# Two graph-attention layers on one core: the planner's durations taken from the profile, layer 0's mask turned over by four transfers instead of one, the last attention but one kept for the end

## The chip, the core and the metric

The kernel runs on one core of a Trainium2 chip. The core has five engines with queues of their own: TensorE (PE, matrix products; its weight loads are shown apart as PEld), VectorE (DVE), ScalarE (ACT), GpSimd (POOL) and SyncE (SP, which here only issues transfers). They meet through semaphores. The metric is the time of one execution on the device, in microseconds (us), of this one core; lower is better.

## What is computed

32 graphs, each with 512 nodes and 512 features per node, and an adjacency matrix of 512 x 512 integers, drawn sparse. Everything is float32. Two layers, each with a layernorm and a relu ahead and a residual after:

```python
h = relu(layernorm(x))                        # layer 0
s = leaky_relu(h @ w_src[:, None] + (h @ w_dst)[None, :] + attn_b, 0.2)
attn = softmax(where(adj + eye == 0, -inf, s), axis=-1)
x = x + attn @ h

h = relu(layernorm(x))                        # layer 1
mask = (adj > 0) | eye
h = elu(gat(h, mask, W1, a_src1, a_dst1, b1, heads=4))   # 512 -> 4 x 256
x = x + gat(h, mask, W2, a_src2, a_dst2, b2, heads=1)    # 1024 -> 512
```

A `gat` projects (`xl = x @ W`), forms `leaky_relu(xl.a_src + xl.a_dst)` for each pair of nodes and each head, sets pairs outside the mask aside, takes the softmax over the sources and multiplies with `xl`.

## The kernel before

**Tiles.** 512 nodes are four tiles of 128 rows. A graph has one layer-0 attention, a projection with W1, four heads' attentions, an elu, a projection with W2 and a last attention. Each projection is made of seven products of half-size blocks instead of eight (`products`, L848 to L915): sums of blocks are formed ahead on DVE or POOL (`combine`, L881/L882), each product is 128 x 257 or 258 in a bank of PSUM (`acc`), and is copied out by ACT or DVE (`evict`, L539/L541 on ACT, L545/L547 on DVE: the writes to `pair` and `xl`) or added to what is there by DVE (L913). The weights carry two more columns with the sums W.a, made at the start (L384 the dot products on DVE, L488 sums on POOL), so that a projection also yields the scores.

**An attention.** Its weights are made in `edge_weights` (L634 to L676). For every tile of 128 rows: the largest neighbour's score of each row (L643, on DVE, 128 x 512, with a mask), then the bound of the row's exponent, `z` (L649) and `m` (L651), both 128 x 4. PE turns that `m` over to lie along a row and spreads it (`spread`, L506, `acc<-ident,col`), ACT forms the leaky relu (L665), DVE subtracts `m` (L668), POOL adds the mask (L671), ACT takes the exponential (L674), PE aggregates (L684). For this each mask is needed twice, with sources in rows and with sources in columns: `m0` and `m0T`, `m1` and `m1T`. Scores of 4, 8 or 16 rows go through PE (L605), are copied to a row, stored in DRAM (`lines`, L611) and read back spread to all partitions (`row_of`, L621; L631 puts a row into a bank).

**Masks.** `masks0` (L751) loads the adjacency by POOL's queue (L725), adds the unit matrix (L758), makes it 0 or a large negative (L761), and turns it over by `transposed_mask` (L729, issue at L735 on SP's queue). `transposed_mask(m, mT, whole)` does it by one transfer when `whole`, else by four, one per tile of rows. The one transfer leaves the result in the order tile, block, column, and `mask_row` (L745) therefore reads it with a stride; four transfers put blocks `mT[:, :, t]` in place, and rows are read without. `masks1` is the like for layer 1.

**The order of work.** Nothing is ordered by hand. The functions record operations in a `Plan`: engine or engines to choose from, a cost (occupied, there) in ns for each, and what is read and written. `Plan.run` (L90) makes list schedules (`draft`), in which each engine takes the operation of the best rank that is due; buffers of limited number (`slots`, L325 on) and a lock between DVE and POOL hold operations back. It tries several weights of looking ahead, derives ranks from the latest times of a schedule, makes the next, and keeps the schedule that ends first by its own costs. All engines then issue in that order. So a cost that is changed can change the whole order and the engine an operation runs on, while the operations stay the same. The costs are in `on_pe` to `by_turning` (L235 to L268) and beside single operations.

**The main program** (L1074 to L1111) records graph 0's and 1's layer 0 first with the constants, then for each graph the masks, the projection, the last attention of the graph before, the heads, the next graph's layer 0 and the second projection. `EARLY` says how many of the four tiles of the last attention but one are recorded ahead of the last projection.

Of the kernel before, what the change touches and what calls it, by code (L numbers as in the profile page):

```python
# [245 lines left out]

def on_act(n, per_partition=0):

    one = n / 1.2 + (95.0, 140.0, 280.0)[per_partition]
    return one, one + 60.0  # L250


def on_pool(n, narrow=False):
# [15 lines left out]
def kernel(  # L269
# [24 lines left out]
    nc = tc.nc  # L294
    B, N, D = x.shape
    H, F = att_src1.shape
# [6 lines left out]
    W2 = (2 + D) // 2  # L303
# [136 lines left out]
    def scores_1(att):  # L440
        for k in range(KD):
            for h in range(H):
                q, kk = QUARTER[k // (KD // 2)][h % 2], k % (KD // 2)
                for i in range(2):
                    op(
                        "DVE", on_dve(F),
                        lambda w=w1_s[q][:, kk, h // 2, :], i=i, h=h: dot(
                            w[:, 2:], flat(att[0])[:, i * HF + h * F : i * HF + (h + 1) * F], w[:, i : i + 1]
                        ),
                        W["w1"]((q, kk)) + att[0](i), W["w1"]((q, kk, h // 2, i)), -LATER, lock=True,  # L450
                    )

    def scores_2(att):
        part = const.tile([P, KH, 2], F32, name="part")
        for k in range(KH):
            (q, r), kk = QUARTER[k // (KH // 2)], k % (KH // 2)
            lo, hi = w2_s[q][:, kk, :], w2_s[r][:, kk, :]
            for i in range(2):
                op(
                    "DVE", on_dve(W2),  # L460
                    lambda lo=lo, i=i, k=k: dot(lo[:, 2:], flat(att[1])[:, i * D : i * D + W2 - 2], part[:, k, i : i + 1]),
                    W["w2"]((q, kk)) + att[1](i), W["w2"](("part", k)), -LATER, lock=True,
                )
                op(
                    "DVE", on_dve(W2),
                    lambda lo=lo, hi=hi, i=i: dot(hi, flat(att[1])[:, i * D + W2 - 2 : (i + 1) * D], lo[:, i : i + 1]),
                    W["w2"]((r, kk)) + att[1](i), W["w2"]((q, kk, i)), -LATER, lock=True,
                )
            op(
                "DVE", on_dve(2), lambda lo=lo, k=k: nc.vector.tensor_add(lo[:, :2], lo[:, :2], part[:, k, :]),  # L470
                W["w2"]((q, kk, 0), (q, kk, 1), ("part", k)), W["w2"]((q, kk, "a")), -LATER,
            )
# [62 lines left out]
    def evict(src, dst, src_of, dst_of, n, bias=None, psum_half=False):  # L535

        def by_act():
            if bias is None:
                nc.scalar.copy(dst_of(), src_of())  # L539
            else:  # L540
                nc.scalar.activation(dst_of(), src_of(), AF.Identity, bias=bias)  # L541

        def by_dve():
            if bias is None:
                nc.vector.tensor_copy(dst_of(), src_of())  # L545
            else:
                nc.vector.tensor_scalar(dst_of(), src_of(), -1.0, None, op0=ALU.add)  # L547

        op(("ACT", "DVE"), (on_act(n, bias is not None), on_dve(n)), (by_act, by_dve), src, dst)

    def turned(values_of, src, place, results_of, dst):

        e = Buffer("row")
        op(
            "ACT", (1040.0, 1100.0),
            lambda: nc.scalar.copy(
                e.at.bitcast(U16).rearrange("p (b f) -> p b f", b=2), values_of().bitcast(U16).rearrange("p (f b) -> p b f", b=2)
            ),  # L560
            src + place, e(0),
        )
        op(
            "SP", by_turning(4 * P * N),
            lambda: nc.sync.dma_start(
                values_of().bitcast(U16).rearrange("p (c n) -> p c n", n=P), e.at.bitcast(U16), transpose=True
            ),
            e(0), src,
        )

        def pair():
            out = results_of()
            k, t = out.shape[1], out.shape[2]
            nc.scalar.copy(
                out.bitcast(U16).rearrange("p k t (n b) -> p k t n b", b=2),
                values_of().bitcast(U16).rearrange("p (b t k n) -> p k t n b", b=2, k=k, t=t),
            )

        op("ACT", (1160.0, 1220.0), pair, src, dst)

    def spread(part, col_of, ahead):

# [51 lines left out]
    def edge_weights(kind, scores, ac, lines, k, mask_max, mask, near):  # L634


        a_of = lambda t: ac.at[:, k, t : t + 1]
        a_row = spread(scores, a_of, AHEAD) if lines is None else in_bank(row_of(lines, k))
        amax, z, m = Buffer("col"), Buffer("col"), Buffer("col")
        for t in range(T):  # L640
            op(
                "DVE", on_dve(N + 60),
                lambda t=t: nc.vector.tensor_tensor_reduce(  # L643
                    by_blocks(junk), mask_row(mask_max, t), by_blocks(a_row.at), 1.0, LOWEST, ALU.add, ALU.max,
                    accum_out=amax.at[:, t : t + 1],
                ),
                a_row(*ROW) + mask_max(*ROW), amax(t),
            )
        op("DVE", on_dve(T), lambda: nc.vector.tensor_add(z.at, ac.at[:, k + 1, :], amax.at), scores + amax(*ROW), z(0))  # L649
        op(  # L650
            "DVE", on_dve(T), lambda: nc.vector.scalar_tensor_tensor(m.at, z.at, SLOPE, z.at, op0=ALU.mult, op1=ALU.max),  # L651
            z(0), m(0),
        )

        E = Buffer(kind)
        m_row = (
            spread(m(0) + E("place"), lambda t: m.at[:, t : t + 1], AHEAD) if near
            else in_bank(row_of(in_lines(lambda: m.at, m(0), 1), 0))
        )
        c_of = lambda t: ac.at[:, k + 1, t : t + 1]  # L660
        c_row = spread(scores + E("place"), c_of, AHEAD) if lines is None else row_of(lines, k + 1)
        for t in range(T):
            op(
                "ACT", on_act(N, 1),
                lambda t=t: nc.scalar.activation(E.at[:, t, :], c_row.at, AF.Prelu, bias=a_of(t), scale=1.0, alpha=SLOPE),  # L665
                c_row(*ROW) + scores, E(t),
            )
            op("DVE", on_dve(N), lambda t=t: nc.vector.tensor_sub(E.at[:, t, :], E.at[:, t, :], m_row.at), m_row(*ROW) + E(t), E(t))  # L668
            op(
                "POOL", on_pool(N, True),  # L670
                lambda t=t: nc.gpsimd.tensor_add(by_blocks(E.at[:, t, :]), by_blocks(E.at[:, t, :]), mask_row(mask, t)),  # L671
                E(t) + mask(*ROW), E(t), lock=True,
            )
            op("ACT", on_act(N), lambda t=t: nc.scalar.activation(E.at[:, t, :], E.at[:, t, :], AF.Exp), E(t), E(t))  # L674
        return E
# [42 lines left out]
    def load_adj(b, m):  # L718

        first, early = not START.wrote, len(adj_loads) < 3
        adj_loads.append(b)
        op(
            "POOL", (1100.0, 5500.0) if first else (2200.0, 16000.0 if early else 8000.0), lambda: nc.gpsimd.dma_start(m.at, node_tiles(adj, b)),  # L725
            () if first else START(0), m(*ROW) + (START(0) if first else []),
        )

# [15 lines left out]

    def mask_row(mask, t):  # L745

        if mask.kind in ("m0T", "m1T"):
            return mask.at.rearrange("p a (b n) -> p a b n", n=P)[:, :, t, :]
        return by_blocks(mask.at[:, t, :])

    def masks0(b):  # L751


        m0, m0T = Buffer("m0"), Buffer("m0T")
        load_adj(b, m0)
        for t in range(T):
            own = lambda t=t: m0.at[:, t, node_block(t)]
            op("DVE", on_dve(P), lambda own=own: nc.vector.tensor_add(own(), own(), ident), m0(t), m0(t), lock=True)  # L758
        op(
            "DVE", on_dve(T * N, 4.0),  # L760
            lambda: nc.vector.tensor_scalar(m0.at, m0.at, 0.0, NO_EDGE, op0=ALU.is_equal, op1=ALU.mult),  # L761
            m0(*ROW), m0(*ROW), lock=True,
        )
        transposed_mask(m0, m0T, True)
        return m0, m0T

    def masks1(b):
# [18 lines left out]
    def layer0_scores(b):  # L786
        rstd, nmr = layernorm(X[b])
        h0, ac = Buffer("h"), Buffer("ac")
        for t in range(T):
            relu_normed(h0, X[b], t, rstd, nmr)  # L790
            for i, w in ((1, ws_r), (0, wd_r)):
                op(
                    "DVE", on_dve(D), lambda t=t, w=w, i=i: dot(h0.at[:, t, :D], w, ac.at[:, i, t : t + 1]),
                    h0(t) + W["w0"](0, 1), ac((i, t)), lock=True,
                )
        c = ac(*((1, t) for t in ROW))
# [274 lines left out]

    EARLY = 1  # L1074
    load_x(0)
    att = load_constants()
    layer0_scores(0)
# [61 lines left out]
```

## Time and profile before

| | us |
|---|---|
| median of three runs | 3646.97 (3645.85 to 3647.93) |
| profiled execution, its own time | 3648.51 |
| its span in the profile | 3646.7 |
| PE busy (matmul instructions 16852) | 3542.6, 97% |
| PE weight loads | 3036.1, 83% |
| DVE busy | 2851.2, 78% |
| ACT busy | 2264.6, 62% |
| POOL busy | 1424.6, 39% |
| matmuls of the attentions, L684 | 920.4 + 491.2 + 447.9 in their three largest groups |

The mean clock that PE was granted is 0.994 of full. An engine's line in the profile says when its instructions ran, and a wait names the instruction of another engine (or the transfer) that released it. A busy share is a mean over the whole run. The run has a start of some 150 us, in which constants are loaded and the first graph has no other to work beside, then graphs of about 110.8 us each that look alike, and an end of some 100 us without further graphs.

### The profile page before, as it was taken

The numbers are of one execution on the slowest core, as the hardware profiler recorded it, in microseconds if no ns is written. First come the engines' busy times: TensorE is split into PE (matmuls) and PEld (weight loads), VectorE is DVE, ScalarE is ACT, GpSimd is POOL, SyncE is SP. The second block draws the span as 40 slices with busy tenths as digits, with TensorE's granted clock in tenths as the row PEclk, the third lists the DMA queues.
The fourth block names the chain that finished last, engine by engine and source line by source line (L and its number), as shares of the span: only waits on it lengthen the run. The fifth ranks groups of instructions, "written<-read, shape, count | busy, mean of one in ns | idle before, by whom it ended". The sixth has DMA issues, their size and how long they took to land.

```text
span 3646.7 us, 50543 instructions
## 1 busy us (share of the span) xinstructions
PE 3542.6 (97%) x16852; PEld 3036.1 (83%) x16852; DVE 2851.2 (78%) x7367; ACT 2264.6 (62%) x3929; POOL 1424.6 (39%) x1279
## 2 busy tenths in 40 slices
PE   4899999999999999999999999999999999999998
PEld 3788888888888888888888888888888888888887
DVE  7978778877778877778787788877787877887755
ACT  2666566665666665666666667655666656666554
POOL 4534334434334343334343344343343433343422
PEclk9999999999999999999999999999999999999999
DMA  6244433444433444334443334443334443344321
GB/s 172 77 105 119 104 92 104 100 121 113 96 96 103 104 121 112 90 96 105 115 116 98 95 103 99 125 116 86 97 110 105 119 108 89 103 103 118 105 73 41
DMA packets 510374, 378.82 MB, mean 104 GB/s; under 512 B 348344, under 2 KB 386976, under 8 KB 510112
## 3 DMA queue, kind: packets, MB, share of 16 engines
q1 hardware_dynamic: 476320, 342.03, 32.8%
q0 software_dynamic: 33792, 33.56, 6.1%
q8 instruction: 132, 2.16, 0.2%
q14 instruction: 130, 1.06, 0.1%
HBM read 257.16 MB, written 68.01 MB: 89 GB/s over the span
## 4 chain that ended last, share of the span: by engine, by line
PE 80%; DVE 14%; ACT 2%; issue 1%; DMA 1%; POOL 0%; DVEq 0%; ACTq 0%; SPq 0%
PE acc L684 45%; PE acc L900 32%; DVE junk L384 5%; PE acc L506 3%; DVE v L1013 1%; DVE hT L881 1%; DVE hT L545 1%; DVE col L521 1%; DVE col L649 1%; ACT h L529 1%; DVE v L973 1%; PE acc L605 1%; DVE junk L643 1%; DVE E L881 1%; DVE xl L913 1%
## 5 line engine op out<-in xcount | busy, mean ns | idle before, releaser
L684 PE MATMUL acc<-pair,E 128*128 128x257 f32 x4096 | 920.4, 379 | 2.4 <-ACT row L987 2.4
L684 PEld LDWEIGHTS acc<-pair,E 128*128 128x128 f32 x4096 | 771.7, 189 | 115.5 <-ACT row L987 2.8
L671 POOL TENSOR_TENSOR E<-E,m 128x512 f32<-128x512 f32 x512 | 605.1, 1211 | 455.3 <-DVE E L668 396.7
L900 PE MATMUL acc<-w_T,E 128*128 128x257 f32 (+1 forms) x2048 | 517.9, 380 | 0.8 <-POOL w_T L488 0.8
L684 PE MATMUL acc<-h,E_one 128*128 128x256 f32 (+1 forms) x2048 | 491.2, 381 | 8.6 <-ACT E_one L674 7.5
L684 PE MATMUL acc<-xl,E_one 128*128 128x257 f32 x1984 | 447.9, 381 | 2.7 <-ACT E_one L674 2.7
L643 DVE CUSTOM_DVE_ANT_0 junk<-m1T,acc 128x512 bf16<-128x512 bf16 x640 | 436.6, 682 | 11.4 <-PE acc L506 3.4
L900 PEld LDWEIGHTS acc<-w_T,E 128*128 128x128 f32 x2048 | 385.4, 189 | 61.0 <-POOL w_T L488 1.5
L684 PEld LDWEIGHTS acc<-h,E_one 128*128 128x128 f32 x2048 | 380.8, 191 | 63.6 <-ACT E_one L674 8.3
L684 PEld LDWEIGHTS acc<-xl,E_one 128*128 128x128 f32 x1984 | 371.8, 190 | 54.7 <-ACT E_one L674 3.1
L674 ACT ACTIVATE E<-E 128x512 f32<-128x512 f32 x512 | 315.6, 623 | 161.7 <-POOL E L671 161.4
L913 DVE TENSOR_TENSOR pair<-acc,pair 128x258 f32<-128x258 f32 (+1 forms) x390 | 165.4, 426 | 293.7 <-PE acc L900 219.2
L539 ACT COPY pair<-acc 128x258 f32<-128x258 f32 (+1 forms) x456 | 165.8, 370 | 320.5 <-PE acc L900 315.8
L665 ACT ACTIVATE E<-row,ac 128x512 f32<-128x512 f32 x512 | 341.1, 707 | 2.4 <-DMA row<-lines 2.4
L668 DVE TENSOR_TENSOR E<-E,acc 128x512 f32<-128x512 f32 x512 | 330.4, 678 | 6.5 <-PE acc L506 3.1
L671 POOL TENSOR_TENSOR E_one<-E_one,m0T 128x512 f32<-128x512 f32 x128 | 144.4, 1152 | 355.6 <-DVE E_one L668 355.6
L725 POOL DMA_DIRECT2D m<-in_adj_dram x64 | 51.5, 805 | 590.8 <-DVE col L643 540.7
L900 PE MATMUL acc<-w,hT 128*128 128x258 f32 x1024 | 265.5, 384 | 0.6 <-issue 0.5
L900 PE MATMUL acc<-w,E 128*128 128x257 f32 (+1 forms) x1024 | 264.2, 380 | 0.0
L702 DVE SCALAR_TENSOR_TENSOR x<-acc,r,x 128x256 f32<-128x256 f32 x512 | 239.7, 479 | 30.9 <-PE acc L684 22.8
L529 ACT ACTIVATE h<-x,col,col 128x512 f32<-128x512 f32 x256 | 187.6, 804 | 109.0 <-DVE col L521 109.0
L539 ACT COPY xl<-acc 128x257 f32<-128x257 f32 x218 | 77.6, 369 | 284.9 <-PE acc L900 284.8
(113 smaller groups left out, 6171.9 us busy)
## 6 DMA issues: line engine op xcount, KB each, us to landing
row<-lines SPq DMA_DIRECT2D x442, 256.0 KB, 3.4
x<-in_x_dram SPq DMA_DIRECT2D x32, 1024.0 KB
m<-in_adj_dram POOLq DMA_DIRECT2D x64, 512.0 KB, 6.3
spill<-x SPq DMA_DIRECT2D x32, 1024.0 KB, 4.2
x<-spill SPq DMA_DIRECT2D x32, 1024.0 KB
out_dram<-x SPq DMA_DIRECT2D x30, 1024.0 KB, 4.2
v<-row SPq DMA_TRANSPOSE x192, 2.7
out_dram<-x SPq DMA_DIRECT2D x8, 256.0 KB, 2.0
```

The source lines that it names most:

```text
L384: nc.vector.scalar_tensor_tensor(junk[:, : vector.shape[1]], values, 1.0, vector, op0=ALU.mult, op1=ALU.mult, accum_out=out)
L529: lambda: nc.scalar.activation(h.at[:, t, :D], X.at[:, t, :], AF.Relu, bias=nmr.at[:, t : t + 1], scale=rstd.at[:, t : t + 1]),
L539: nc.scalar.copy(dst_of(), src_of())
L643: lambda t=t: nc.vector.tensor_tensor_reduce(by_blocks(junk), mask_row(mask_max, t), by_blocks(a_row.at), 1.0, LOWEST, ALU.add, ALU.max, a ...
L665: lambda t=t: nc.scalar.activation(E.at[:, t, :], c_row.at, AF.Prelu, bias=a_of(t), scale=1.0, alpha=SLOPE),
L668: op("DVE", on_dve(N), lambda t=t: nc.vector.tensor_sub(E.at[:, t, :], E.at[:, t, :], m_row.at), m_row(*ROW) + E(t), E(t))
L671: lambda t=t: nc.gpsimd.tensor_add(by_blocks(E.at[:, t, :]), by_blocks(E.at[:, t, :]), mask_row(mask, t)),
L674: op("ACT", on_act(N), lambda t=t: nc.scalar.activation(E.at[:, t, :], E.at[:, t, :], AF.Exp), E(t), E(t))
L684: lambda s=s: nc.tensor.matmul(acc.at[:, :n], E.at[:, s, node_block(t)], of(s), start=(s == 0), stop=(s == T - 1)),
L702: lambda acc=acc, r=r, f=f, t=t: nc.vector.scalar_tensor_tensor(X.at[:, t, f], acc.at[:, :HD], r.at, X.at[:, t, f], op0=ALU.mult, op1=ALU. ...
L900: lambda k=k: nc.tensor.matmul(acc.at[:, :width], at[a]()[:, k, node_block(r)], weight_of(w, k, c), start=(first and k == 0), stop=(k == n ...
L913: op("DVE", on_dve(width), lambda: nc.vector.tensor_add(place(), acc.at[:, :width], place()), acc(0) + token, token)
```

## The change

It does the following:

- changes the costs that the planner uses: an ACT operation with a bias or scale per partition 140 to 186 ns beside its elements, and 130 instead of 60 ns until its result is there; a plain copy by ACT (`on_act_copied`) 52 ns beside its elements and 160 until there; dot products 125 elements longer; the two elu turns of ACT 945 and 1062 ns instead of 1040 and 1160; the row maximum L643 50 elements shorter; the first adjacency load 11000 instead of 5500 ns;
- turns `m0` over by four transfers of 128 x 512 instead of one of 128 x 2048; `m0T`'s rows are then read without a stride. `m1` stays with one;
- sets `EARLY` to 0, so that all four tiles of the last attention but one are recorded after the last projection.

The operations are otherwise the same. The diff, with hunks of the same kind left out:

```diff
-    one = n / 1.2 + (95.0, 140.0, 280.0)[per_partition]
-    return one, one + 60.0
+    one = n / 1.2 + (95.0, 186.0, 280.0)[per_partition]
+    return one, one + 130.0
+
+
+def on_act_copied(n):
+    one = n / 1.2 + 52.0
+    return one, one + 160.0
...
-                        "DVE", on_dve(F),
+                        "DVE", on_dve(F + 125),
...
-        op(("ACT", "DVE"), (on_act(n, bias is not None), on_dve(n)), (by_act, by_dve), src, dst)
+        op(("ACT", "DVE"), (on_act_copied(n) if bias is None else on_act(n), on_dve(n)), (by_act, by_dve), src, dst)
...
-            "ACT", (1040.0, 1100.0),
+            "ACT", (945.0, 1100.0),
...
-        op("ACT", (1160.0, 1220.0), pair, src, dst)
+        op("ACT", (1062.0, 1220.0), pair, src, dst)
...
-                "DVE", on_dve(N + 60),
+                "DVE", on_dve(N + 10),
                 lambda t=t: nc.vector.tensor_tensor_reduce(
...
-            "POOL", (1100.0, 5500.0) if first else (2200.0, 16000.0 if early else 8000.0), lambda: nc.gpsimd.dma_start(m.at, node_tiles(adj, b)),
+            "POOL", (1100.0, 11000.0) if first else (2200.0, 16000.0 if early else 8000.0), lambda: nc.gpsimd.dma_start(m.at, node_tiles(adj, b)),
...
     def mask_row(mask, t):
 
-        if mask.kind in ("m0T", "m1T"):
+        if mask.kind == "m1T":
             return mask.at.rearrange("p a (b n) -> p a b n", n=P)[:, :, t, :]
         return by_blocks(mask.at[:, t, :])
...
-        transposed_mask(m0, m0T, True)
+        transposed_mask(m0, m0T)
         return m0, m0T
...
-    EARLY = 1
+    EARLY = 0
```

The lines of the changed kernel lie five further down from the ACT costs on.

More of the change, by code (lines that the diff above doesn't have):

```diff
@@ L459, in scores_2 @@
                 op(
-                    "DVE", on_dve(W2),
+                    "DVE", on_dve(W2 + 125),
                     lambda lo=lo, i=i, k=k: dot(lo[:, 2:], flat(att[1])[:, i * D : i * D + W2 - 2], part[:, k, i : i + 1]),
@@ L464, in scores_2 @@
                 op(
-                    "DVE", on_dve(W2),
+                    "DVE", on_dve(W2 + 125),
                     lambda lo=lo, hi=hi, i=i: dot(hi, flat(att[1])[:, i * D + W2 - 2 : (i + 1) * D], lo[:, i : i + 1]),
@@ L792, in layer0_scores @@
                 op(
-                    "DVE", on_dve(D), lambda t=t, w=w, i=i: dot(h0.at[:, t, :D], w, ac.at[:, i, t : t + 1]),
+                    "DVE", on_dve(D + 125), lambda t=t, w=w, i=i: dot(h0.at[:, t, :D], w, ac.at[:, i, t : t + 1]),
                     h0(t) + W["w0"](0, 1), ac((i, t)), lock=True,
```

## The prediction

> **What bounds the kernel now.** I read the page's busy shares first, then the chain that ended last, then what TensorE (PE) waits for over the whole run and by stage, and last one steady graph instruction by instruction. The page:
>
> ```profile
> PE 3542.6 (97%) x16852; PEld 3036.1 (83%) x16852; DVE 2851.2 (78%) x7367; ACT 2264.6 (62%) x3929; POOL 1424.6 (39%) x1279
> PE 80%; DVE 14%; ACT 2%; issue 1%; DMA 1%; POOL 0%; DVEq 0%; ACTq 0%; SPq 0%
> ```
>
> PE is busy 97% of the span and holds 80% of the chain. It has the same 16852 instructions to do after the change, so only its idle time can change; the other engines matter where PE waits for them. The waits of PE over the run (line waited for: us in total, times, longest):
>
> ```profile
> PE acc L506 <- DVE col L651: 23.8, 30, 4.4
> PE acc L506 <- DVE junk L384: 21.9, 4, 18.8
> PE acc L684 <- ACT E_one L674: 13.0, 4, 4.1
> PE acc L605 <- DVE ac L798: 10.2, 4, 9.3
> PE acc L506 <- DVE v L1013: 9.8, 30, 1.9
> ```
>
> All of them come to 96 us. By stage: about 58 us in the first 200 us, 26 us in 200 to 3400 (28 waits for L651, together 16.3; 28 for L1013, together 6.8), 12 us after that. So there are two kinds: a start, once, and a small wait that returns with every graph. One graph in the middle takes 110.82 us, as the windows say (us; PE, PEld, DVE, ACT, POOL busy and instructions; clock; DMA share; GB/s):
>
> ```profile
> 0.00:50.00 50.00, 19.72 (x76) 15.47 (x76) 32.11 (x105) 9.15 (x13) 20.02 (x24) 1.00 0.92 236
> 50.00:100.00 50.00, 31.82 (x127) 24.83 (x127) 46.91 (x138) 16.79 (x35) 25.99 (x21) 0.83 0.36 99
> ...
> 1314.05:1424.87 110.82, 109.87 (x527) 94.43 (x526) 87.91 (x226) 70.88 (x123) 43.30 (x39) 1.00 0.39 106
> ```
>
> In that graph PE waits once for L651, 0.6 us: it is about to turn the four numbers per row that set the softmax bound (col, L649/L651) and VectorE (DVE) hasn't written them. DVE's work up to that point:
>
> ```profile
> 1320.52 0.43 DVE L913 TENSOR_TENSOR pair<-acc,pair 128x258 f32<-128x258 f32 x1 [0.44 <-PE acc L900]
> 1321.79 2.48 DVE L668 TENSOR_TENSOR E_one<-E_one,acc 128x512 f32<-128x512 f32 x4 [0.84 <-ACT acc L631]
> 1324.19 0.68 DVE L643 CUSTOM_DVE_ANT_0 junk<-m1T,acc 128x512 bf16<-128x512 bf16 x1
> ...
> 1343.24 1.07 DVE L649 TENSOR_TENSOR col<-ac,col 128x4 f32<-128x4 f32 x1
> ```
>
> The last idle gap of DVE there ends at 1321.79; from it to the L651 at 1345.38 DVE runs nearly without a gap for 23.6 us: the second group of four subtractions (L668), twelve of the row maxima (L643), and what lies between. One wait in that stretch is another engine's doing: L649 takes 1.07 us where the same line takes 0.15 elsewhere, and ends when GpSimd's (POOL) group of four ends:
>
> ```profile
> 1339.78 4.51 POOL L671 TENSOR_TENSOR E<-E,m 128x512 f32<-128x512 f32 x4 [5.56 <-DVE E L668]
> ```
>
> At the start, DVE holds the first layernorm behind the mask's load, and PE holds a project behind the second graph's scores (the 9.3 us above):
>
> ```profile
> DVE m L758 <- DMA m<-in_adj_dram: 5.5, 1, 5.5
> ```
>
> **What the Trainium skill says.** "Perfetto Trace Analysis", Identifying the Most-Contended Engine: matmul busy time is a poor measure of distance to the roofline, weight-load busy time a better one. Here that is 83% beside 97%; but the steady graph spends 109.87 of 110.82 us on PE's rows, and its passes of 0.217 us (42 in 9.09 us) do not shorten by waiting less, so what is to be had in the steady stage is under 1 us a graph. "SBUF — State Buffer", SBUF: two separate sides: a VectorE instruction with two SBUF inputs and a GpSimd instruction take an exclusive lock on a shared port pair, and the later one blocks. The trace agrees: L649 has two SBUF inputs, started 0.08 us into POOL's last subtraction and took 1.07 instead of 0.15 us. "DMA: Bandwidth & Descriptors", Queues, rings and completion order: each DMA engine consumes one queue's descriptors in ring order. The trace of before fits that: on SP's queue the m0T transfer was issued at 17.40 to 25.3 us behind the w1 loads, and the loads issued after it landed after it (b_r at 30.4).
>
> **The change, part by part.** The profiled execution is 3648.51 us, its span 3646.7, with 1.8 around it; it lies 1.54 over the median of 3646.97. I sum against 3648.51 and subtract 1.54.
>
> *Costs alone* change no instruction. They change which order the planner keeps, so I compared the order of instructions on each engine. PE's order over a graph is the same but for shifts of under 2 us, and 29 graphs are alike. Moved: 88 evictions of a product (pair<-acc) from ACT (370 ns) to DVE (425 ns), 31 small ones (ac<-pair) from ACT to DVE, 29 row evictions (278 ns) from DVE to ACT; some additions change places between POOL and DVE. DVE gains 88 x 0.425 + 31 x 0.2 - 29 x 0.28 = 35 us, 1.2 a graph. Against 110.82 - 87.91 = 22.9 us idle a graph that is nothing, if it falls into the idle part. It does not:
>
> *Where the new DVE evictions stand.* In before, the second L668 group starts 7.74 us into the graph (counted from 1314.05, PE's turn of ac). In after, two of the added evictions stand directly ahead of it on DVE, one of them for a product that PE ends only at 7.90. It then starts at about 7.90 + 0.43 + 0.2, some 8.6: 0.9 late. What is queued behind it is the whole unbroken stretch. The sum of DVE's instructions from there to the third L651 is 22.62 us in both orders; in before it took 23.6 with the lock, and POOL's group that causes it is released by the same DVE stretch, so it moves along. Third col ready: 8.6 + 22.62 + 1.0 = 32.2. PE gets there at 30.8 in both. Wait 1.4 instead of 0.58, which I take as 1.3: **+0.72**. The fourth col, at 30.55 from the start of the stretch instead of 30.92, is due at 38.8 on PE, 0.9 earlier than in before (39.6), plus the 1.3 and 0.2 of waits ahead: ready 8.6 + 30.55 + 1.5 (what contention had added by then in before) = 40.7 against 40.3: **+0.35**. First col: 8.6 + 5.9 = 14.5, exactly PE's 14.51: **+0.1**. Unknown on both sides: if the collision is missed, the third wait is 0.4 and the sum is below nothing (-0.2); if both are late in full, +1.6.
>
> *The v transposes* (L506 waiting for L1013): the second now stands 65.62 into the graph rather than 64.32, with three more matmuls in front. The wait of 6.8/28 goes: **-0.24** a graph. Next late is nothing near it.
>
> Steady: 0.72 + 0.35 + 0.1 - 0.24 = 0.93, x 28 = **+26 us** (bounds -0.3 x 28 = -8 to 1.6 x 28 = +45).
>
> *L643 priced at N + 10.* The planner now thinks 614 ns for what takes 0.73 from start to start in the timeline (1337.29, 1338.02): twelve of them make 1.4 us it doesn't see. That may be why it lets the stretch begin later; no cost beyond the above.
>
> *m0T by four transfers.* SP spends 1.6 us on one 128x2048 and 1.23 on a 128x1024 in the steady stage; 128x512 isn't shown, I extrapolate 1.05, so 4.2 instead of 1.6, +2.6 us of SP a graph. In the order two of the four stand ahead of the row transfers that head scores need, which are put back by 0.7 to 1.8 us. Cover: SP is idle most of the graph, and ACT doesn't wait for rows in it; if that were gone, up to 1.8 x 28 = 50 us. I take 0. POOL reads m0T in 1.152 us and m in 1.211, so contiguous rows bring nothing to it; DVE's L643 on m0T gets a plain stride, which no row prices apart.
>
> *The start.* Gain: DVE's layernorm now stands ahead of the mask: the 5.5 us wait goes, and is not on the way any more. Loss: the four m0T transfers now stand on SP behind x1, b, att2 and w2 (4.5 MB, at the 286 GB/s that the saturated stretch shows 15.6 us after w1's last landing at 25.8), so m0T lands at about 42 to 43.5; a POOL weight sum that needs w2 stands ahead of the mask product as well. First attention on PE at about 45 instead of 33.6: **+11.5**. Against it: DVE does nine weight dots, x1's statistics and m1's mask in that wait, and PE's project no longer has the second graph's turn ahead of it: the 9.3 goes (**-9.3**), and the two following waits, for E_one (4.1) and row (2.4), which that DVE backlog made: **-6.5**. Sum **-4.3** (bounds: +11.5 if nothing is made up; -12 if m0T comes 8 us sooner than I think).
>
> *The end.* With the last-but-one attention wholly after the last project in the program, its four tiles lie in the same place in PE's order as before; two matmuls (0.87 us) less between the last v turns. **+0.5** (-1 to +3).
>
> Sum: 26 - 4.3 + 0.5 = +22.2; 3648.51 + 22.2 - 1.54 = **3669.2**.
>
> **The rivals.**
>
> *Faster, through the same point.* If the second L668 group does not start later than about 7.9, or the lock falls elsewhere, the third col is ready by 31.0 to 31.2 and PE's wait is at most what it is now. For it: one of two added evictions is of a product that DVE waited for anyway, and DVE had a 0.84 us gap there for ACT's L631. Against it: PE's end at 7.90 is in the order. Then -0.24 for v and -0.3 for col are left: -0.54 x 28 = -15, start -4.3: 3648.51 - 19 - 1.54 = 3628. The point of decision is the third L651 31.4 us after PE's turn of ac.
>
> *The start decides.* The steady stage is even, and m0T behind the constants costs its 11.5 unmade: 3658.
>
> *It doesn't do what it says.* Losses at the col offset gains at the start and at v: 3647. For it: PE's work is the same and 26 us is all the steady waiting there is.
>
> **How the numbers follow.** Col stall grows (3669): 0.56, its own range 3652 to 3694. Faster (3628): 0.24. Start (3658): 0.10. Even (3647): 0.10. About 0.2% (7.3 us) is what a measurement of this kernel can tell from no change. Slower: 0.50 of the first, 0.08 of the third, 0.58. Same: 0.06 + 0.01 + 0.02 + 0.08 = 0.17. Faster: 0.23 + 0.02 = 0.25. The range takes in the faster case to its middle: 3628 to 3694.
>
> **What would show it.** Right: 28 waits of PE for L651 in the steady stage, near 1.3 us each and some for the fourth col; none for L1013; a second L668 group near 8.6; no L758 wait and no 9.3 us wait at the start; first attention near 45 us. Wrong: waits for L651 of 0.5 us or less, a period under 110.8, or PE waiting for ACT's edge weights because rows come late.

## The result, and the profile after

The changed kernel takes 3654.42 us (median of twelve runs, 3652.33 to 3657.73) against 3646.95 before (twelve runs, 3645.59 to 3650.36): a ratio of 1.002, 95% interval 1.0013 to 1.0028, so 7.5 us slower; the two sets of runs don't overlap. I had forecast 22 us. The profiled execution took 3655.71 us, its span 3653.9. Lines stand five further down than before: L656 is the L651 of before, L673 L668, L626 L621.

The first line of the changed kernel's page, then the waits of PE over its run that bear on the forecast (line waited for: us in total, times, longest):

```profile
PE 3542.3 (97%) x16852; PEld 3029.3 (83%) x16852; DVE 2822.9 (77%) x7425; ACT 2252.2 (62%) x3844; POOL 1473.6 (40%) x1306
```

```profile
PE acc L511 <- DVE col L656: 43.2, 34, 10.7
PE acc L689 <- ACT E_one L679: 23.1, 8, 13.0
PE acc L511 <- DVE junk L389: 16.3, 4, 13.2
PE acc L511 <- ACT h L534: 9.1, 2, 8.3
PE acc L905 <- DVE pair L918: 6.4, 3, 5.4
PE acc L511 <- DVE v L1018: 3.3, 2, 1.8
```

The wait for v has gone from 30 times to 2. In 200 to 3400 us, L656 is waited for 31 times, 27.6 us together, and E_one five times, 4.6 us. To see where the time comes from I measured both profiles at one landmark, PE's first turn of the 16 rows of ac in each graph (acc<-ident,ac 128*16). From the start to graph 1's turn the change is 0.5 us faster (205.65 against 206.17), from there to graph 2's 1.0 slower, over the next 28 graphs 7.4 slower (3113.4 against 3106.0), at the end 0.7 faster: together the 7.2 us between the spans. A graph below is counted from its landmark.

The 28 graphs are not all alike. Half of them take as long as before, 110.8 us, as the third line shows for one; the first two are the start (windows, with the columns of the prediction):

```profile
0.00:50.00 50.00, 9.94 (x33) 7.29 (x34) 34.29 (x101) 9.15 (x13) 18.38 (x23) 1.00 0.95 239
50.00:100.00 50.00, 37.57 (x171) 31.43 (x169) 47.67 (x134) 16.67 (x34) 25.59 (x20) 0.92 0.29 86
871.49:982.30 110.81, 109.95 (x528) 94.33 (x526) 86.73 (x229) 70.36 (x120) 45.15 (x40) 1.00 0.40 105
```

In that graph PE waits once, 0.86 us, where before it waited 0.58 for col and 0.24 for v. The timeline of DVE in that graph shows the two added evictions, the stretch behind them and its end:

```profile
879.63 0.43 DVE L550 COPY pair<-acc 128x258 f32<-128x258 f32 x1 [1.74 <-PE acc L905]
880.09 0.18 DVE L550 COPY ac<-pair 128x16 f32<-128x16 f32 x1
880.18 2.47 DVE L673 TENSOR_TENSOR E_one<-E_one,acc 128x512 f32<-128x512 f32 x4
...
901.10 0.92 DVE L654 TENSOR_TENSOR col<-ac,col 128x4 f32<-128x4 f32 x1
...
902.94 0.19 DVE L656 SCALAR_TENSOR_TENSOR col<-col 128x4 f32<-128x4 f32 x1
```

The loss is in the other half, up to 3 us in a graph. The worst begins at 2316.37 (113.76 us). SP's queue in it, and ACT, which waits for the rows that SP fetches:

```profile
2314.66 0.33 SPq L626 DMA_DIRECT2D row<-lines  x1
2315.04 3.73 SPq L740 DMA_TRANSPOSE m1T<-m  x1
2318.82 0.91 SPq L616 DMA_DIRECT2D lines<-row  x2
2323.37 1.29 SPq L626 DMA_DIRECT2D row<-lines  x3
```

```profile
2327.39 0.59 ACT L636 COPY acc<-row 128x512 f32<-128x512 f32 x1 [3.01 <-DMA row<-lines]
```

SP issues the three row loads only when the stores of those lines have landed, and the stores stand behind m1T's transfer, which holds SP's queue for 3.73 us. ACT gets the row 3 us late, DVE subtracts late, and PE waits 2.56 us for E_one. In before the first of these row loads is issued 2.1 to 3.3 us after the landmark in 26 of 29 graphs; in the changed kernel 3.7 to 5.0 us after it in 25 of 29, in this graph 7.0. As the trace reads, the whole chain on SP is later because PE turns the row of m (acc<-ident,col 128*4) 6.85 us ahead of the landmark instead of 7.62, and the store behind it lands later still. No run moved that turn alone.

### The profile page after: what moved, and what is told of

Read it like the earlier page. It is cut to its first block, busy times and chain, and to the rows that moved or that the text cites. A ratio compares the mean times of both kernels' runs of the same rounds, so it can differ in the third digit from the quotient of the medians.

```text
span 3653.9 us, 50454 instructions
## 1 busy us (share of the span) xinstructions
PE 3542.3 (97%) x16852; PEld 3029.3 (83%) x16852; DVE 2822.9 (77%) x7425; ACT 2252.2 (62%) x3844; POOL 1473.6 (40%) x1306
## 4 chain that ended last, share of the span: by engine, by line
PE 75%; DVE 18%; DMA 3%; issue 2%; ACT 1%; POOL 1%; SPq 0%; DVEq 0%; ACTq 0%
PE acc L905 42%; PE acc L689 30%; DVE junk L648 6%; PE acc L511 4%; DVE E L673 3%; DVE x L707 3%; DMA row<-lines 2%; DVE E_one L673 2%; DVE col L654 1%; POOL E_one L676 1%; DVE junk L389 1%; PE acc L610 0%; DVE v L978 0%; DMA x<-in_x_dram 0%; DVE r L701 0%
## 5 line engine op out<-in xcount | busy, mean ns | idle before, releaser
L676 POOL TENSOR_TENSOR E<-E,m 128x512 f32<-128x512 f32 x512 | 593.5, 1188 | 416.3 <-DVE E L673 349.6
L689 PE MATMUL acc<-h,E_one 128*128 128x257 f32 (+1 forms) x2048 | 479.8, 380 | 16.5 <-ACT E_one L679 16.5
L918 DVE TENSOR_TENSOR pair<-acc,pair 128x258 f32<-128x258 f32 (+1 forms) x390 | 161.6, 423 | 285.5 <-PE acc L905 278.9
L673 DVE TENSOR_TENSOR E<-E,acc 128x512 f32<-128x512 f32 x512 | 337.4, 672 | 5.5 <-PE acc L511 4.2
L544 ACT COPY pair<-acc 128x258 f32<-128x258 f32 (+1 forms) x368 | 137.6, 374 | 302.0 <-PE acc L905 297.5
L905 PE MATMUL acc<-w,E 128*128 128x257 f32 (+1 forms) x1024 | 271.9, 380 | 0.0
L905 PE MATMUL acc<-w,pair 128*128 128x257 f32 x1024 | 253.6, 379 | 0.0
```

The costliest lines, as they stand in the source:

```text
L689: lambda s=s: nc.tensor.matmul(acc.at[:, :n], E.at[:, s, node_block(t)], of(s), start=(s == 0), stop=(s == T - 1)),
L905: lambda k=k: nc.tensor.matmul(acc.at[:, :width], at[a]()[:, k, node_block(r)], weight_of(w, k, c), start=(first and k == 0), stop=(k == n ...
L918: op("DVE", on_dve(width), lambda: nc.vector.tensor_add(place(), acc.at[:, :width], place()), acc(0) + token, token)
```

## The experiments

Every run was timed beside the kernel before, on the same chip. To before: difference of the medians in that comparison, us. Period: mean over the 28 graphs from the third on, us. Waits: the waits of PE that the profile names, us in each of these graphs.

| kernel | median, us | to before | ratio (95%) | period | waits |
|---|---|---|---|---|---|
| before | 3646.95 | | | 110.93 | 0.92 |
| changed | 3654.42 | +7.5 | 1.0013 to 1.0028 | 111.19 | 1.11 |
| a_whole | 3652.22 | +4.3 | 1.0005 to 1.0018 | 111.14 | 1.02 |
| b_apart | 3656.73 | +8.8 | 1.0015 to 1.0032 | 111.24 | 1.12 |
| b_costs | 3653.19 | +5.3 | 1.0008 to 1.0021 | 110.94 | 0.89 |
| a_rows | 3654.65 | +6.7 | 1.0011 to 1.0025 | 111.14 | 1.10 |
| a_both | 3646.76 | -0.4 | 0.9991 to 1.0007 | 110.87 | 0.90 |
| a_start | 3652.40 | +5.2 | 1.0006 to 1.0023 | 111.31 | 1.18 |
| b_early | 3648.30 | +1.1 | 0.9995 to 1.0012 | 110.93 | 0.92 |
| a_bound | 3627.38 | -19.8 | 0.9934 to 0.9959 | 110.17 | 0.33 |
| b_bound | 3625.82 | -21.4 | 0.9927 to 0.9954 | 110.15 | 0.34 |
| a_best | 3645.73 | -1.5 | 0.9986 to 1.0002 | 110.87 | 0.51 |
| a_best4 | 3623.16 | -25.1 | 0.9916 to 0.9943 | 110.11 | 0.31 |
| b_four | 3603.75 | -43.5 | 0.9865 to 0.9892 | 109.29 | 0.00 |
| f_whole | 3602.02 | -45.2 | 0.9859 to 0.9889 | 109.29 | 0.00 |
| f_rmax | 3633.99 | -13.2 | 0.9951 to 0.9977 | 110.68 | 0.42 |
| f_act | 3644.30 | -2.9 | 0.9983 to 1.0000 | 110.71 | 0.42 |
| f_adj | 3632.72 | -14.5 | 0.9950 to 0.9978 | 110.38 | 0.07 |

**The transfers, with the order kept** (a_whole, b_apart). After the planner has chosen, only what the recorded operation issues is exchanged:

```diff
 a_whole, in transposed_mask of the changed kernel (and mask_row with the stride for m0T):
-  mT.at[:, :, node_block(t)] <- m.at[:, t, :], for t in 0 to 3
+  the whole m0T <- m at t = 0, nothing at t = 1 to 3
 b_apart, in transposed_mask of the kernel before (and mask_row without it for m0T):
-  the whole m0T <- m
+  four transfers, one behind the other, at the place of the one
```

> The changed kernel with the order of every engine kept, only layer 0's mask turned over by one transfer again (at the place of the first of the four) and read with a stride. Theory R (rows): the loss in the steady stage is the order's, which puts the row of m through PE 0.8 us later before the turn of ac, and so m1T, the two stores and the three row loads on SP's queue 1.4 us later; the loads then land with no slack, and a late one stops ACT, DVE and PE. It expects no gain: 3652 to 3657 us, with PE's waits for E_one in some graphs. Theory Q (queue): the three more transfers a graph hold up SP's queue and the DMA engines; it expects 3647 to 3649 us and no waits for E_one.

> The kernel before with its order kept, only layer 0's mask turned over by four transfers at the place of the one, and read without a stride. Theory R: no change, 3645 to 3649 us, because the row loads stand ahead of the transfers and have 1.4 us more slack there. Theory Q: slower, 3652 to 3656 us, with PE waiting for E_one or ACT for rows.

Neither theory held alone: the first run came out as R said, the second as Q did. With one transfer the order of the changed kernel still loses 4.3 us, with E_one waited for five times (3.7 us); the excess of single graphs over 0.86 us at col is gone. In before's order the four transfers, which R expected to be free, cost 8.8 us. SP in a graph of before (landmark at 1314.05), then SP and ACT in one of b_apart (landmark at 539.65):

```profile
1321.75 1.60 SPq L735 DMA_TRANSPOSE m0T<-m  x1
1323.45 0.52 SPq L621 DMA_DIRECT2D row<-lines  x1
1324.08 0.38 SPq L611 DMA_DIRECT2D lines<-row  x1
1327.71 1.57 SPq L621 DMA_DIRECT2D row<-lines  x3
```

```profile
547.35 5.64 SPq L738 DMA_TRANSPOSE m0T<-m  x4
553.10 0.52 SPq L621 DMA_DIRECT2D row<-lines  x1
553.72 0.37 SPq L611 DMA_DIRECT2D lines<-row  x1
560.18 4.86 SPq L621 DMA_DIRECT2D row<-lines  x4
```

```profile
558.57 0.59 ACT L631 COPY acc<-row 128x512 f32<-128x512 f32 x1 [4.51 <-DMA row<-lines]
```

The four take SP 5.64 us (the one took 1.60), so the row load directly behind them goes out later: in the median of the 28 graphs 12.9 us after the landmark instead of 9.4. ACT waits for that load in 18 of them, here 4.51 us, and in none of before's. For all rows together ACT waits 114.3 us in these graphs, in before 12.2. DVE waits for ACT, and PE up to 2.3 us for the second col.

The small store behind that load adds to it: the next row load waits until the store has landed. In this graph it is issued 6.5 us after the store (553.72 to 560.18), in the one of before 3.6. This graph is the extreme; the medians are 3.6 and 3.1 us. A store that lands later behind more transfers fits what the Trainium skill says in "DMA: Bandwidth & Descriptors", Queues, rings and completion order: on each DMA engine a queue's descriptors are consumed in order, though a later one may finish ahead of an earlier one.

**The costs alone** (b_costs: the new costs, one transfer, EARLY 1).

> The kernel before with the new costs alone: one transfer for layer 0's mask, EARLY 1. PE's order over a graph is that of the changed kernel. Theory R: the whole loss is in the costs, 3652 to 3657 us, about as the changed kernel. Theory Q: 3647 to 3649 us.

+5.3 us, in R's range but not for R's reason: its profile has 4.5 us of that before graph 1's turn (210.7 against 206.2), and the steady period is before's. The row loads are as late in it as in the changed kernel (3.6 to 5.0 us after the landmark in 26 of 29 graphs). So late row loads alone don't make the steady loss. With the same new costs, the changed kernel's start is 0.5 us faster: a start is another with each plan.

**SP's order** (a_rows, then a_both: the same with one transfer).

```diff
 SP, in each graph
-  m1T<-m; lines<-row x2; row<-lines x3; m0T<-m ...
+  lines<-row x2; row<-lines x3; m1T<-m; m0T<-m ...
```

> The changed kernel with one edit of SP's order: in each graph the transfer of m1T is issued behind the two stores and the three row loads and not ahead of them. Theory R: the rows come some 3 us earlier, ACT no longer waits for them, PE's waits for E_one in the steady stage (4.6 us) and the excess over 0.86 us of those for the third col go: 3645 to 3649 us, a period of 110.81 in all graphs. Theory Q: the same transfers are in the queue, no change beyond 2 us: 3652 to 3656 us. If m1T comes too late, DVE's row maxima (L648) wait for it and it is slower than the changed kernel.

E_one is not waited for any more, as R expected, and yet no time is gained. PE's waits in 200 to 3400 us, with the kernel's own numbering (L687 is L656):

```profile
PE acc L540 <- DVE col L687: 31.3, 34, 1.2
PE acc L540 <- ACT h L563: 0.7, 2, 0.6
```

The waits for col have grown from 27.6 to 31.3 us. A reading is that m1T and the four m0T now stand together ahead of the later row loads. So both edits at once:

> The changed kernel with one transfer for layer 0's mask (read with a stride) and m1T issued behind the three row loads on SP. The four earlier runs leave two rivals. Theory P (two parts): in the changed kernel's order the rows of E_one land without slack (waits for E_one, which the move of m1T took away), and four transfers hold back the row loads behind them (the third wait for col 1.15 in place of 0.86 us, which one transfer took away); each edit alone left or enlarged the other wait. P expects neither wait in the steady stage, a wait of 0.86 us in every graph, and 3646 to 3649 us. Theory O (order): what is left of the loss is the order's own and not a matter of transfers: 3651 to 3654 us, as with one transfer alone.

3646.76 us: P held. Nothing is left of the loss: in the changed kernel's order, the four transfers and m1T's place together make it. PE's waits are those of the regular graphs:

```profile
PE acc L540 <- DVE col L687: 25.6, 31, 0.9
PE acc L540 <- ACT h L563: 0.2, 1, 0.2
```

**The start** (a_start) **and the end** (b_early, EARLY 0 alone).

```diff
 a_start
 SP:   + m0T<-m x4 (graph 0) behind w1's last load, ahead of x1, b, att2, w2
 POOL: + sum that needs w2, power of the second layernorm: behind E_one<-E_one,m0T x4
 DVE:  + bn_stats of x1 behind E_one<-E_one,acc x4
```

> The changed kernel with the start in the order of before in three points: layer 0's first four mask transfers ahead of the second x and the constants of the second layer on SP, the sum that needs w2 and the second layernorm's power behind the four masked sums on POOL, the second x's statistics behind the four subtractions on DVE. First attention on PE near 34 us instead of 44. If the start was held by the mask's transfer, the second graph's turn of ac on PE comes 8 to 10 us earlier and the run is 3644 to 3648 us. If the sums and dot products of the weights hold it, which DVE and POOL do in the wait, it comes within 2 us of where it was (205.6): 3652 to 3657 us.

PE's first attention comes at 30.2 instead of 43.9 us, 13.7 earlier, and graph 1's turn at 202.9 instead of 205.65: less than 3 of it arrive. Most of the time is given back in the next wait, as PE's timeline of this kernel shows:

```profile
30.20 15.99 PE L738 MATMUL acc<-h,E_one 128*128 128x257 f32 x64 [5.67 <-ACT E_one L728]
65.28 1.12 PE L558 MATMUL acc<-ident,h 128*128 128x128 f32 x4 [19.08 <-ACT h L581]
```

In the changed kernel that wait for h is 8.33. The dot products of the weights on DVE, done in the wait there, are still ahead of the second layernorm here. Four of them also take 2.4 to 2.5 us instead of 0.42, each beside a sum of weights on POOL (DVE's timeline):

```profile
45.24 0.42 DVE L435 SCALAR_TENSOR_TENSOR junk<-w,E 128x256 bf16<-128x256 f32 x1
45.59 0.08 DVE L435 DVE_READ_ACCUMULATOR junk<-w,E 128x1 f32 x1
45.71 2.44 DVE L435 SCALAR_TENSOR_TENSOR junk<-w,E 128x256 bf16<-128x256 f32 x1
```

The run's median does not tell the two starts apart (3652.4).

> The kernel before with EARLY 0 alone. Only the last graphs' order differs. My prediction gave the end +0.5 us (-1 to +3): 3646 to 3650 us. If it is a part of the loss, 3650 us or more.

No change that can be told, as forecast.

**Col's place on DVE** (a_bound, b_bound). The two instructions that finish col are moved right behind their last row maximum, where more than four instructions lay between:

```diff
 DVE, third col of a graph of the changed kernel
   junk<-m1T,acc (L648, the last of four)
+  col<-ac,col (L654); col<-col (L656)
   E<-E,acc (L673) x4, x<-acc,r,x (L707) x2, ...
-  col<-ac,col (L654); ...; col<-col (L656)
```

> The changed kernel with one edit of DVE's order: the two small instructions that make col (L654, L656) stand right behind their last row maximum wherever more than four instructions lay between; in the third of a graph they were 3 to 5 us behind it, after four subtractions. If the steady wait of 0.86 us is only these instructions' place, PE's waits for the third col go and 29 x 0.86 = 25 us with them: 3627 to 3633 us, period 109.9 to 110.0. If another chain is right behind (v, ACT's exponentials, rows), the period stays near 110.8 with another name: 3648 to 3655 us.

> The same edit to the kernel before. There the last row maximum ends at 28.5 us in the graph and the col is written at 31.3. If only the place counts: 28 x 0.58 = 16 us less, 3629 to 3633 us, if the waits for v (0.24 a graph) don't grow. If the wait for v takes over what is gained, 3643 to 3648 us.

Both gained what was expected or more: 27.3 us against the changed kernel (its +7.5 became -19.8), and 21.4 us against before. In before's order no wait for col is left, and the waits for v did not grow (7.0 us in all). In the changed order the third col is not waited for any more, but the fourth is, some 0.3 us in nearly every graph (28 waits, 9.2 us). So the steady wait for the third col came from the place of two instructions of 0.15 us.

**All gains together** (a_best; a_best4 with the cols moved only past more than four).

> The changed kernel with all that gained: one transfer for layer 0's mask, m1T behind the three row loads, the start of before in the three points of the earlier run, and col's two instructions right behind the last row maximum in every case. If the gains are apart from each other: 3646.8 for the first two, less 29 x (0.73 + 0.31) = 30 for the cols and 2.7 for the start: 3612 to 3617 us, period 109.8. If a wait behind col is close (v, rows, E_one), 3620 to 3626 us, as with the cols alone.

> As the kernel with all that gained, but col's two instructions are moved only where more than four instructions lay between, as in the run with that edit alone. There the two edits near the second projection, which moved them by two or four places, put them ahead of an eviction and an addition that PE waits for (0.19 us named, 0.3 unnamed in each graph). If that is where the gain went: period 110.1, 3646.8 - 20 - 3 = 3621 to 3626 us. If one of the other edits collides with the cols: near 3645 us again.

a_best missed by about 30 us. Near the second projection, the cols now stood ahead of an addition that PE waits for, in each graph (its timeline on DVE, then on PE; L978 is L918):

```profile
977.14 0.16 DVE L708 TENSOR_TENSOR col<-ac,col 128x4 f32<-128x4 f32 x1
977.34 0.16 DVE L710 SCALAR_TENSOR_TENSOR col<-col 128x4 f32<-128x4 f32 x1
977.42 0.42 DVE L978 TENSOR_TENSOR pair<-acc,pair 128x258 f32<-128x258 f32 x1
```

```profile
977.89 0.70 PE L965 MATMUL acc<-w_-T,hT 128*128 128x258 f32 x2 [0.19 <-DVE pair L978]
```

Without those moves it is 3623.16 us. PE's pauses, counted as further down, are then 0.88 us a graph instead of 1.68, and the period is shorter by as much.

**The four transfers alone, planned** (b_four, old costs), and that order with one transfer (f_whole).

> The kernel before with the four transfers alone, planned as such at the old costs, so that the planner sees four operations on SP and can put row loads between them. Four transfers at the place of the one cost 8.8 us. If the planner's own order finds them a place where nothing waits: 3646 to 3650 us; if SP's time and the late rows remain whatever the place: 3652 to 3657 us.

> The kernel with the four transfers planned at the old costs (3603.75 us), its order kept on every engine, but one transfer issued at the place of the first of the four and read with a stride. If that kernel's gain lies in the order (its third turn of col stands 0.8 us later on PE and no wait is left): 3602 to 3606 us. If it lies in the transfers or in the reading without a stride: 3640 us or more.

The largest effect of the study, 43.5 us faster than before, which no theory had. And it isn't the transfers: with one transfer in the same order it is 45.2 us faster than before. PE's waits in 200 to 3400 us of f_whole, and a stretch as long as one period:

```profile
PE acc L506 <- DVE col L651: 0.2, 1, 0.2
```

```profile
860.00:969.28 109.28, 109.28 (x528) 94.66 (x527) 85.11 (x229) 69.91 (x121) 44.21 (x39) 1.00 0.42 107
```

PE's third turn of col stands 0.8 us later in that order (31.6 us after the landmark at 865.08 in b_four, where before reached it at 30.8), and DVE has col by 31.2:

```profile
896.10 0.14 DVE L651 SCALAR_TENSOR_TENSOR col<-col 128x4 f32<-128x4 f32 x1
```

```profile
896.66 0.60 PE L506 MATMUL acc<-ident,col 128*128 128x128 f32 x4
```

Giving the planner four operations changed more than SP's queue: DVE has 7423 instructions instead of 7367 and ACT 3874 instead of 3929, and the third L649, 1.07 us in before, takes 0.15 or 0.16 in all 28 graphs.

**One new cost each, on top of b_four** (f_rmax: `on_dve(N + 60)` to `on_dve(N + 10)`; f_act: `on_act` and `on_act_copied`; f_adj: 5500 to 11000 for the first adjacency load).

> The four transfers at the old costs with one new cost, that of the row maximum (N + 10 in place of N + 60). Theory V (value): the low price makes DVE's stretch too long for the turns of col; then 3630 to 3650 us. Theory T (turn): any edit makes another order, and its time follows from where PE's third turn of col stands and when DVE starts the stretch; here the turn stands at 31.4 us after that of ac, as in the kernel of 3603.75 us, and no added eviction stands right ahead of the stretch: 3600 to 3615 us.

> The four transfers at the old costs with ACT's new costs alone (per partition, latency, plain copies). V: the cheaper and later copies spoil the order: 3630 to 3650 us. T: the third turn stands at 31.0 us, the stretch's sum is 0.4 us shorter than in before, one added eviction ahead of it: waits near 0, 3603 to 3622 us.

> The four transfers at the old costs with one new cost that concerns the start alone: the first adjacency load at 11000 instead of 5500. V: a cost of one operation at the start can't matter in the steady graphs: 3600 to 3610 us. T: the order of all graphs is another; the third turn stands at 31.0 us and the two added evictions of the changed kernel are ahead of the stretch: a wait of some 0.4 us a graph, 3618 to 3640 us.

f_rmax fell to V's range and f_adj to T's; f_act went out of T's range into V's. Neither theory stands. A cost of one operation at the start alone changed the steady graphs and made the kernel 29 us slower than b_four, so V's reason, the value, isn't enough. The waits for col do not tell the time either: there are 3 of them in f_adj (1.1 us) and 6 in f_rmax (6.4 us). Their periods are longer by pauses of PE that no wait names (f_adj: 110.38 less 0.07 of waits, against 109.29).

**PE's pauses, from its starts.** The traces show where these pauses are. This is the turn of before that waits for col, with the row of passes ahead of it:

```profile
1339.49 5.36 PE L684 MATMUL acc<-pair,E 128*128 128x257 f32 x24
1345.44 0.65 PE L506 MATMUL acc<-ident,col 128*128 128x128 f32 x4 [0.58 <-DVE col L651]
```

The 24 passes start 0.217 us apart, which makes 5.20 us; the turn starts 5.95 after the first of them. So PE loses 0.75 us where 0.58 is named. A pass is shown 0.38 us long, so the first 0.16 us of a pause lie under its end. I took the distance of each start from the one before it and counted what goes more than 0.04 us beyond the usual one (0.216 or 0.217 us behind a pass, 0.109 behind a turn). That makes 1.72 us a graph in before, 1.95 in the changed kernel, 0.94 in b_bound, 1.15 in f_adj, 1.41 in f_rmax, 1.48 in f_act and 0.07 in b_four and f_whole. The period less these pauses is 109.2 to 109.3 us in every kernel of the table, so the periods differ by PE's pauses. In before they stand at the turns of col (0.75), of v (0.40) and of the scores ac (0.30, of which 0.02 is named). In f_adj the largest part, 0.55 us, stands at the turns of h, which wait for ACT's layernorm.

## Why the prediction was right or wrong

The direction and the range (3628 to 3694) held; the size was three times too large, and the direction held by luck. Two steps failed. The steady sum at col, 0.72 + 0.35 + 0.1 a graph, was to make the kernel slower; in the regular graphs it came to 0.28, which the wait for v takes back. And the transfers of m0T, which I took as 0, have a part in the steady loss that did come, 7.4 us. Its sign stands in the prediction among those of being wrong: PE waits for ACT's edge weights because rows come late (E_one, five times). In detail:

- *Where the evictions stand*: the second group of subtractions was forecast at 8.6 us after the landmark, it is at 8.69. What failed is the term that followed: 22.62 + 1.0 for the stretch. It takes 22.95 us (880.18 to 903.13). The lock on L654 was there (0.92 us instead of 0.14), but the forecast sum of the other instructions was some 0.4 us too long. So the third wait grew by 0.28, not 0.72; the fourth col, which I had late by 0.35, and the first are not waited for in the regular graphs. (The fourth is, once the third is not: a_bound.)
- *The wait for v* went as forecast, -0.24. With it a regular graph is even, 110.81 against 110.83. The +26 of the sum was 0.
- *m0T by four transfers*: "I take 0" failed. The SP time was 5.0 us (two pairs of 2.50), not 4.2: a transfer of 128x512 holds SP 1.26 us, no less than the 1.23 that I took for twice the size. The cover I named, that ACT doesn't wait for rows, holds less in the changed kernel: in the 28 graphs ACT waits for rows 47 times (29.7 us), in before 13 times (12.2). In before's order the step costs 8.8 us. In the changed order it makes the steady loss together with m1T's place ahead of the row loads, which I did not price as a step at all: with both edited (a_both) the kernel is at before's time. Why b_costs, with one transfer, m1T in that place and rows as late, has no steady loss stays open.
- *The start*: first attention forecast at 45, measured 43.9; the 9.3 went as forecast. But the two waits I struck out (6.5) came back as others (5.4 for pair, 8.3 instead of 6.0 for h): -0.5 by graph 1's turn instead of -4.3.
- *The end*: +0.5 forecast, -0.7 measured in the profiles, and nothing in the medians.
- *What bounds it*: I wrote that under 1 us a graph was to be had in the steady stage. f_whole takes 1.65. The 109.87 us that PE seemed busy in before held pauses: they are 1.72 us a graph, and 0.92 of waits is named.
- The rival that the start decides did not come, nor the faster one, though an order with hardly a wait was near: the new costs left out (b_four).

Left open: why the planner's search ends at an order with hardly a pause with the old costs and four transfers, and what in the new costs spoils it. Each of the three that were tried does, at different turns; the others were not tried.

## What to carry to other kernels

When a planner sets the order, a cost that is corrected does not make one place better but draws a new plan; compare plans on the chip and keep the order of the best one (here 3602.02 us), instead of trusting that truer costs give a better one. Price transfers on an in-order queue with what stands behind them: here the row loads, and the small stores that other loads wait for, made them dear. Judge PE's waiting by the distance of its starts, since the named waits show only a part. A short instruction that releases the bounding engine belongs right behind its last input, but only where nothing more urgent waits on that engine.

## What I had not expected of the hardware

How long a transposing transfer holds SP's queue hardly follows from its size here: 1.26 us for m0T's 128x512, 1.6 for m0T's 128x2048, and 3.0 for m1T's 128x2048, medians of the changed kernel and of before; why m1T's is longer stays open. A wait of PE costs more than its idle time: taking 0.58 us of named waiting a graph out of before (b_bound) shortened the mean period by 0.78 us. And the lock between DVE and POOL, which the Trainium skill tells of in "SBUF — State Buffer", SBUF: two separate sides, falls on small instructions too: the third L649 of before takes over 1.0 us instead of 0.15 in all 28 graphs and ends with POOL's addition of the mask (the prediction calls it a subtraction); L654 of the changed kernel takes 0.91 to 0.98.
